# A causal mask as one rank-64 product of staircases instead of two 64-column products, in a transformer layer on one core

## The chip, the core and the metric

The kernel runs on one core of a Trainium2 chip. A core has a matrix engine (TensorE, PE in the profile; its weight loads are PEld), three engines for elementwise work (VectorE or DVE, ScalarE or ACT, GpSimd or POOL), and SyncE (SP), which here issues nearly all DMA transfers. Each engine works through its own list of instructions in order and waits on semaphores for the others. TensorE writes to PSUM only; the other data lie in SBUF. The metric is the device time of one execution in microseconds, as a median over runs.

## The reference

A transformer layer on two sequences of 2048 positions with 256 features: layer norm, causal attention with 16 heads of 16 features and rotary embedding, then layer norm and a gated feed-forward block with inner size 704, whose operands are rounded to a 4-bit grid in blocks of 16.

```python
q, k = (rope(q), rope(k))
scale = math.sqrt(HEAD_D)
att = jnp.einsum('bhqd,bhkd->bhqk', q, k) / scale
mask = jnp.tril(jnp.ones((t, t), dtype=bool))
att = jnp.where(mask, att, -jnp.inf)
att = jax.nn.softmax(att, axis=-1)
y = jnp.einsum('bhqk,bhkd->bhqd', att, v)
...
x = x + _L0_attn_ref(_layernorm(x, axis=-1), ...)
x = x + _L0_ffn_ref(_layernorm(x, axis=-1), ...)
```

Everything is float32. The part that matters here is the mask: a query may not see a later key.

## The kernel before

A sequence is cut into chunks of 512 positions (CH), four per sequence, each of four tiles of 128. The heads are taken in groups of four (GROUP), so there are 2 sequences x 4 chunks x 4 groups = 32 slots. Each slot runs two passes over the keys seen so far.

The maximum pass (`max_steps`) computes scores with queries on the partitions. A step is one query tile i, one key chunk kc and one pair of heads d: the two heads h lie in partitions 0 to 63 and 64 to 127 (`strips`, STRIP = 64), each with its query and key split into leading and trailing parts, so that a product contracts over 64 rows of the array. Both heads' products (L1094) go to two PSUM banks, and VectorE reduces each bank to a row maximum (L1118). Where the key chunk is the query's own, only (i + 1) x 128 columns are made, and the last 128 of them hold the causal triangle.

The exponential pass (`value_steps`) computes the scores again with keys on the partitions: a product that subtracts the maxima (L1227), the scores on top (L1235), and for the four key tiles of the chunk itself the triangle on the first 128 columns; ScalarE takes the exponential (L1250), and the values are multiplied with it (`weigh`, L1283), in column strips of 32.

The triangle is added on TensorE by `masked` (L1059). It accumulates on top of the scores a product of the triangle tile with a selecting identity. Since a strip has 64 rows, one product can select 64 columns, so each head takes two weight loads and two products of 64 columns (L1062). The tiles are `mask_q` for the maximum pass and `mask_k`, its mirror, for the exponential pass; both are bfloat16, filled with -1.0e30 or 0 by `triangle` on GpSimd (L377, L380) and narrowed on VectorE (L391). `pick` holds the two identities (L408).

The order of the whole program is laid by a planner. Each piece of work is added with an engine, an assumed cost, the things it reads and writes and a due time (`Plan.add`, L147), and `Plan.ordered` (L187) simulates the engines, keeps the buffers' limits (ROOM), and gives the sequence in which the pieces are written out; `in_order` (L505) then ties each engine to that sequence. The feed-forward steps of earlier chunks, the projections of the next chunk and the rounding of the weights are interleaved with the attention steps in this way. A different assumed cost can therefore move any piece. The planner also counts a penalty when TensorE changes between the tilings "strip" (64 rows), "value" (32 columns) and "whole".

In the first 170 us of the plan (KEPT), where the planner sees TensorE idle, `kept_busy` (L484) puts in filler products of 256 columns that have no use but to keep the engine running, one for each 0.2 us of planned idle time (FILLER). Their moving operand is `mask_q`, so none is put in before the planner sees that tile ready (L1901).

The set-up work of the start (`begun`, from L1831) has due times written by hand: `lay_mask_q` at -8.2, `lay_pick` at -8.1, `lay_mask_k` at -7.0 after the weights of the values.

Of the kernel before, what the change touches and what calls it, by code (L numbers as in the profile page):

```python
# [46 lines left out]
AUG = HD + 1  # L47
ROPE_BASE = 2500
LN_EPS = 1e-5
NEG = -1.0e30  # L50
CH = 512
TPC = CH // P
BLOCK = 16
# [261 lines left out]
def layer_kernel(  # L315
# [48 lines left out]
    make_identity(nc, ident)  # L364


    def triangle(name, sign):

        t, thing, full = const.tile([P, 2, P], BF16, name=name), Thing(), []

        def step(due, after=()):
            temp = Thing("x1")

            def filled():
                full.append(ffn.tile([P, E], F32, tag="x1", name="tri", bufs=ROOM["x1"]))
                wide = full[0].rearrange("p (h q) -> p h q", h=2)
                nc.gpsimd.memset(wide, 0.0)  # L377
                for strip in range(2):
                    part = wide[strip * STRIP : (strip + 1) * STRIP]
                    nc.gpsimd.affine_select(  # L380
                        out=part,
                        in_=part,
                        compare_op=ALU.is_ge,
                        fill=NEG,
                        base=0,
                        pattern=[[-sign * STRIP, 2], [sign, P]],
                        channel_multiplier=-sign,
                    )

            def narrowed():  # L390
                nc.vector.tensor_copy(t.rearrange("p h q -> p (h q)"), full[0])  # L391

            add(POOL, 1.2, filled, after, [temp], due)
            add(DVE, 0.33, narrowed, [temp], [thing], due)

        return t, thing, step


    mask_q, mask_q_, lay_mask_q = triangle("mask_q", 1)
    mask_k, mask_k_, lay_mask_k = triangle("mask_k", -1)  # L400
    pick = const.tile([P, STRIP], BF16, name="pick")
    pick_ = Thing()

    def lay_pick(due):
        def run():
            for strip in range(2):
                rows = slice(strip * STRIP, (strip + 1) * STRIP)
                nc.vector.tensor_copy(pick[rows], ident[rows, rows])  # L408

        add(DVE, 0.5, run, [fixed], [pick_], due)  # L410


    less = [const.tile([P, P], BF16, name=f"less{d}") for d in range(2)]
    less_ = Thing(), Thing()
# [69 lines left out]
    def kept_busy(bank):  # L484

        while spare[0] >= FILLER:
            spare[0] -= FILLER
            nc.tensor.matmul(
                bank[:, : 2 * P],
                lhsT=ident_b,  # L490
                rhs=mask_q.rearrange("p h q -> p (h q)"),
                start=True,
                stop=True,
            )
# [561 lines left out]
    def strips(t, h, *rest):  # L1056
        return t[(slice(STRIP * h, STRIP * (h + 1)), *rest)]

    def masked(sc, h, col, mask):  # L1059
        for half in range(2):  # L1060
            at = STRIP * half
            nc.tensor.matmul(  # L1062
                sc[h][:, col + at : col + at + STRIP],
                lhsT=strips(mask, h, half),
                rhs=strips(pick, h),
                start=False,
                stop=(half == 1),
            )

    order = [(b, c) for b in range(B) for c in range(NC)]  # L1070
    maxima, max_ = {}, {}
# [3 lines left out]
    def max_steps(b, c, g):  # L1075
# [7 lines left out]
        def one(i, kc, d, due):  # L1083
            duo = 2 * (g % 2) + d
            cols = CH if kc < c else (i + 1) * P
            ps, got = (Thing("ps"), Thing("ps")), []

            def run():
                qT = qTs[b, c, g]
                kT = kTs[b, kc, g // 2]  # L1090
                sc = [ps_s.tile([P, CH], F32, tag="ps", name="sc") for _ in range(2)]
                kept_busy(sc[0])
                for h in range(2):
                    nc.tensor.matmul(  # L1094
                        sc[h][:, :cols],
                        lhsT=strips(qT, h, d, slice(i * P, (i + 1) * P)),
                        rhs=strips(kT, h, duo, slice(0, cols)),
                        start=True,
                        stop=(kc < c),
                    )  # L1100
                if kc == c:
                    for h in range(2):
                        masked(sc, h, cols - P, mask_q)
                got.append(sc)

            def reduced(h):
                name = "parts" if c else "mx"
                if name not in st:
                    st[name] = att.tile(
                        [P, TPC, 2, 2, NC] if c else [P, TPC, 2, 2],  # L1110
                        F32,
                        tag=name,
                        name=name,
                        bufs=1 if c else 2,
                    )
                at = st[name][:, i, h, d]
                dst = at[:, kc : kc + 1] if c else at.unsqueeze(1)
                nc.vector.tensor_reduce(dst, got[0][h][:, :cols], AX.X, ALU.max)  # L1118

            add(  # L1120
                PE,
                0.18 + 0.44e-3 * cols if kc == c else 0.27,
                run,
                [qT_[b, c, g], k_[b, kc, g // 2][g % 2], mask_q_, pick_],
                [*ps, m_order],
                due,
                [parts if c else mx],
                "strip",
                FEED_M,
                0.07,  # L1130
            )
            for h in range(2):
                own = Thing(of=parts if c else mx)
                found.append(own)
                add(DVE, on_vector(cols), lambda h=h: reduced(h), [ps[h]], [own], due)
# [67 lines left out]
    def value_steps(b, c, g):  # L1203
# [9 lines left out]
        def score(j, d, due):  # L1213
            off = offset(j)
            duo = 2 * (g % 2) + d
            jj = (j % TPC) * P
            ps, got = (Thing("ps"), Thing("ps")), []
            ex_[j, d] = Thing("ex")

            def run():  # L1220
                qT = qTs[b, c, g]
                kT = kTs[b, j // TPC, g // 2]
                mT = maxima[b, c, g]
                sc = [ps_s.tile([P, CH], F32, tag="ps", name="sx") for _ in range(2)]
                kept_busy(sc[0])
                for h in range(2):
                    nc.tensor.matmul(  # L1227
                        sc[h][:, off:],
                        lhsT=strips(less[d], h),
                        rhs=strips(mT, h, slice(off, CH)),  # L1230
                        start=True,
                        stop=False,
                    )
                for h in range(2):
                    nc.tensor.matmul(  # L1235
                        sc[h][:, off:],
                        lhsT=strips(kT, h, duo, slice(jj, jj + P)),
                        rhs=strips(qT, h, d, slice(off, CH)),
                        start=False,
                        stop=(j < TPC * c),  # L1240
                    )
                if j >= TPC * c:
                    for h in range(2):
                        masked(sc, h, off, mask_k)
                got.append(sc)

            def exponential(h):
                if (j, d) not in st:
                    st[j, d] = exps.tile([P, 2, CH], F32, tag="ex", name="ex")
                nc.scalar.activation(  # L1250
                    st[j, d][:, h, off:], got[0][h][:, off:], AF.Exp, scale=HD**-0.5
                )

            cols = CH - off
            add(
                PE,
                0.455 if j < TPC * c else 0.14 + 0.75e-3 * cols,
                run,
                [qT_[b, c, g], k_[b, j // TPC, g // 2][g % 2], max_[b, c, g], mask_k_, pick_, less_[d]],
                [*ps, e_order],  # L1260
                due,
                [ex_[j, d]],
                "strip",
                FEED_V,
                0.22,
            )
            parts = ex_[j, d].parts = [Thing(of=ex_[j, d]) for _ in range(2)]
            for h in range(2):
                add(ACT, on_scalar(cols), lambda h=h: exponential(h), [ps[h]], [parts[h]], due)
# [574 lines left out]
    def transpose_biases(due):  # L1844
# [18 lines left out]
        (-8.6, lambda due: lay_bias(bvb, bv, bvb_, due)),  # L1863
        (0.4, lambda due: lay_bias(bob, bo, bob_, due)),
        (-8.8, lay_spread),
        (-8.2, lay_mask_q),
        (-8.1, lay_pick),
        (-7.3, lay_ident_b),
        (-7.2, lambda due: lay_less(0, due)),
        (-7.1, lambda due: lay_less(1, due)),  # L1870
        (-7.0, lambda due: lay_mask_k(due, [wv_])),
        (
            -7.6,
            lambda due: add(
# [23 lines left out]
        step(at)  # L1898
    plan.near_end = end - NEAR
    for t in plan.ordered():  # L1900
        if t.engine == PE and (t.end < KEPT or t.start > plan.span - ENDING) and ident_b_.there_by(t.start) and mask_q_.there_by(t.start):  # L1901
            spare[0] = t.idle
        t.run()
        spare[0] = 0.0
        in_order(t.end < DAWN)
# [62 lines left out]
```

## Time and profile before

| what | value |
|---|---|
| median of 3 runs | 1381.62 us (1381.47 to 1383.63) |
| span of the profiled execution | 1378.9 us |
| mean granted clock of TensorE | 0.979 of full speed |
| instructions of TensorE: products, weight loads | 10408, 10408 |
| of these L1062, the mask | 1024 in the maximum pass, 1024 in the exponential pass |
| fillers (L488) | 139, from 5.0 to 161.5 us |
| first scores product | 23.82 us |

The profiled execution is one run; its span goes from the first to the last instruction of the program. "Busy" of an engine is the union of its instructions' times; TensorE's products are pipelined, and each record lasts from its start to a modelled end, so records overlap. The chain is the work that ended last, followed back step by step to what released it. In the groups by form, a row gives line, engine, operation, names (written<-read), the tile of the array where it is not the whole (64*128 is 64 rows by 128 columns), the shape of the moving operand, the count, then busy time, mean duration in ns, and the idle time before. In the timeline, a row gives start and length in us, then engine, line, operation, names, shape, count, and the idle time before it with the releaser in brackets; equal neighbours are merged. In the table by stretch, a row gives the stretch, its length, then busy time and count for PE, PEld, DVE, ACT and POOL, the granted clock, the share of the DMA engines and GB/s.

### The profile page before, as it was taken

The page shows a single profiled execution, that of the slowest core. Times are in us where ns is not written, and L with a number is a line of the kernel's source. Part 1 is how long each engine was busy: PE and PEld are TensorE (multiplying, and loading weights), DVE is VectorE, ACT ScalarE, POOL GpSimd, SP SyncE. Part 2 cuts the span into 40 slices and gives each one's busy share as a digit, 9 for nine tenths or more (in the row PEclk, how much of TensorE's full clock was granted, in tenths as well). Part 3 has the DMA queues.
Part 4 walks back from the last instruction along what each step waited for, and adds up shares of the span by engine and source line. Part 5 has one row for each costly group of instructions (what it writes and reads, how often), then busy time and mean ns, then how long its engine had stood idle before and what let it go on. Part 6 is the DMA issues. An engine that isn't in the chain of part 4 may idle for free.

```text
span 1378.9 us, 27730 instructions
## 1 busy us (share of the span) xinstructions
PE 1317.6 (96%) x10408; PEld 656.7 (48%) x10408; DVE 1115.1 (81%) x2415; ACT 749.9 (54%) x1670; POOL 538.4 (39%) x685
## 2 busy tenths in 40 slices
PE   7988999999999999999998999999999999999977
PEld 4544444444544444444454555444454444444445
DVE  7788989988889998875479888996878988894296
ACT  2542655556555566557643455554655566667711
POOL 4754634434423334314345644432442332320360
PEclk8998999999999999999999999999999999999988
DMA  2653432411221401221343414240130130000000
GB/s 88 133 134 100 103 94 58 104 33 55 62 41 44 107 20 41 64 45 51 89 113 94 108 44 97 66 95 22 47 86 17 43 81 13 9 9 9 9 1 19
DMA packets 61887, 84.39 MB, mean 61 GB/s; under 512 B 14772, under 2 KB 30520, under 8 KB 61752
## 3 DMA queue, kind: packets, MB, share of 16 engines
q1 hardware_dynamic: 61744, 82.61, 24.2%
q8 instruction: 82, 1.34, 0.4%
q14 instruction: 53, 0.43, 0.1%
q10 hardware_dynamic: 8, 0.00, 0.0%
HBM read 55.09 MB, written 27.49 MB: 60 GB/s over the span
## 4 chain that ended last, share of the span: by engine, by line
PE 65%; DVE 19%; POOL 5%; issue 5%; DMA 3%; ACT 2%; SPq 0%; POOLq 0%; DVEq 0%; ACTq 0%
PE av L1283 15%; PE sc L1094 9%; PE pg L1575 9%; PE sx L1227 8%; DVE parts L1118 7%; PE sx L1235 7%; PE pd L1669 6%; PE pj L837 3%; PE pth L1434 2%; PE po L1519 1%; PE pv L1019 1%; DVE scale L582 1%; DVE step L609 1%; DVE mx L1118 1%; PE sc L1062 1%
## 5 line engine op out<-in xcount | busy, mean ns | idle before, releaser
L1250 ACT ACTIVATE ex<-sx 128x512 f32<-128x512 f32 (+3 forms) x1280 | 592.8, 538 | 345.9 <-PE sx L1235 202.1
L1118 DVE TENSOR_REDUCE parts<-sc 128x1 f32<-128x512 f32 (+3 forms) x1152 | 637.9, 611 | 65.2 <-PE sc L1094 46.6
L1235 PE MATMUL sx<-qT,kT 64*128 64x512 f32 (+3 forms) x1280 | 335.6, 521 | 0.0
L1283 PE MATMUL av<-ex,v 128*32 128x512 f32 (+3 forms) x2560 | 301.3, 543 | 0.0
L1094 PE MATMUL sc<-kT,qT 64*128 64x512 f32 (+3 forms) x1280 | 280.3, 425 | 8.9 <-DMA kT<-parts 2.5
L1227 PE MATMUL sx<-mT,less 64*128 64x512 bf16 (+3 forms) x1280 | 246.5, 355 | 5.4 <-DVE parts L1118 1.6
L1094 PEld LDWEIGHTS sc<-kT,qT 64*128 64x128 f32 x1280 | 132.8, 188 | 168.1 <-DVE parts L1118 51.2
L1227 PEld LDWEIGHTS <-less 64*128 64x128 bf16 x1280 | 66.5, 94 | 213.3 <-issue 205.5
L590 POOL TENSOR_SCALAR inv<-inv 128x16 f32<-128x16 f32 (+2 forms) x82 | 17.7, 216 | 373.0 <-DVE inv L586 341.2
L1235 PEld LDWEIGHTS sx<-qT,kT 64*128 64x128 f32 x1280 | 131.3, 196 | 9.0 <-issue 6.8
L1669 PE MATMUL pd<-wdT,hrT 128*128 128x256 f32 (+1 forms) x384 | 103.9, 411 | 1.5 <-ACT hrT L1438 1.0
L1283 PEld LDWEIGHTS av<-ex,v 128*32 128x32 f32 x2560 | 52.6, 108 | 70.8 <-issue 60.4
L1669 PEld LDWEIGHTS pd<-wdT,hrT 128*128 128x128 f32 (+1 forms) x384 | 70.4, 197 | 29.1 <-issue 16.0
L889 POOL TENSOR_TENSOR t<-t,cs 128x512 f32<-128x512 f32 x31 | 39.9, 1286 | 110.2 <-DVE t L883 104.8
L1575 PE MATMUL pg<-wgT,xT 128*128 128x352 f32 x224 | 76.9, 476 | 0.9 <-ACT xT L1438 0.8
L837 PE MATMUL pj<-xnT,wqkT 128*128 128x512 f32 x128 | 73.8, 672 | 3.5 <-DVE v L1028 1.7
L1118 DVE TENSOR_REDUCE mx<-sc 128x1 f32<-128x128 f32 (+3 forms) x128 | 54.3, 477 | 25.8 <-PE sc L1062 25.8
L1575 PE MATMUL pg<-wuT,xT 128*128 128x352 f32 x224 | 74.4, 471 | 0.1
L1062 PE MATMUL sc<-pick,mask_q 64*128 64x64 bf16 x1024 | 67.3, 198 | 0.0
L615 POOL TENSOR_TENSOR h<-h,step 128x704 f32<-128x704 f32 x28 | 47.2, 1686 | 48.8 <-DVE step L612 41.0
L1601 ACT ACTIVATE h<-pg 128x352 f32<-128x352 f32 x64 | 29.9, 467 | 64.6 <-PE pg L1575 56.5
L547 POOL TENSOR_SCALAR ve<-mv 128x1 f32<-128x1 f32 x64 | 12.6, 197 | 130.4 <-DVE mv L543 127.1
(163 smaller groups left out, 1614.8 us busy)
## 6 DMA issues: line engine op xcount, KB each, us to landing
qT<-parts SPq DMA_DIRECT2D x120, 128.0 KB
kT<-parts SPq DMA_DIRECT2D x120, 128.0 KB
parts<-high SPq DMA_DIRECT2D x30, 256.0 KB
parts<-t SPq DMA_DIRECT2D x30, 256.0 KB
sums<-avs SPq DMA_DIRECT2D x28, 256.0 KB
cs<-in_rope_dram SPq DMA_DIRECT2D x8, 512.0 KB
xin<-in_L_attn_x_dram SPq DMA_DIRECT2D x28, 128.0 KB
y<-sums SPq DMA_DIRECT2D x28, 128.0 KB
```

Source lines behind the costliest of these rows:

```text
L615: queue.tensor_tensor(src(), src(), st["step"], ALU.add)
L837: nc.tensor.matmul(got["pj"], lhsT=wqkT[:, k, i, cols], rhs=xnTs[b, c][:, k, :], start=(k == 0), stop=(k == KE - 1),)
L889: (nc.gpsimd if early and i == 0 else queue).tensor_tensor(swapped, swapped, angles[b, c][:, 1, :], ALU.mult)
L1062: nc.tensor.matmul(sc[h][:, col + at : col + at + STRIP], lhsT=strips(mask, h, half), rhs=strips(pick, h), start=False, stop=(half == 1),)
L1094: nc.tensor.matmul(sc[h][:, :cols], lhsT=strips(qT, h, d, slice(i * P, (i + 1) * P)), rhs=strips(kT, h, duo, slice(0, cols)), start=True, ...
L1118: nc.vector.tensor_reduce(dst, got[0][h][:, :cols], AX.X, ALU.max)
L1227: nc.tensor.matmul(sc[h][:, off:], lhsT=strips(less[d], h), rhs=strips(mT, h, slice(off, CH)), start=True, stop=False,)
L1235: nc.tensor.matmul(sc[h][:, off:], lhsT=strips(kT, h, duo, slice(jj, jj + P)), rhs=strips(qT, h, d, slice(off, CH)), start=False, stop=(j ...
L1250: nc.scalar.activation(st[j, d][:, h, off:], got[0][h][:, off:], AF.Exp, scale=HD**-0.5)
L1283: nc.tensor.matmul(st["av"][SLOT * s : SLOT * (s + 1), off:], lhsT=v[:, at : at + SLOT], rhs=st[j, d][:, h, off:], start=(j == 0), stop=(j ...
L1575: nc.tensor.matmul(got[half], lhsT=split("xrT")[:, k, :], rhs=wT[:, k, half * IH : (half + 1) * IH], start=(k == 0), stop=(k == KE - 1),)
L1669: nc.tensor.matmul(st["pd"], lhsT=st["hrT"][:n, k, :], rhs=wdT[:n, k, :], start=(k == 0), stop=(k == KI - 1),)
```

## The change

The two triangle tiles and the two identities are replaced by one bfloat16 tile `stairs` of two halves, for each strip of 64 rows. In row e, the first half, over positions q, is 2^80 for q <= 2e, 1 for q = 2e + 1, and 2^-80 beyond. The second half, over positions k, is -2^40 for k >= 2e + 2, -2^-40 for k = 2e + 1, and -2^-120 before. The product of the two, summed over the 64 rows, is at most -2^40 wherever k > q and between -2^-34 and 0 elsewhere. One product of 128 columns per head thus adds the whole triangle. In the maximum pass the first half is the stationary operand and the second the moving one; in the exponential pass they change places.

The tile is made by two memsets of 128 columns and eight selects of 64 x 128 on GpSimd, and one cast on VectorE, with due time -8.2. The fillers read `stairs`. The planner's assumed costs of a masked step fall by 0.065 us in the maximum pass and by 0.04 us in the exponential pass.

```diff
-NEG = -1.0e30
+STEEP = 80
+LOW = 40
...
-    def triangle(name, sign):
...
-    mask_q, mask_q_, lay_mask_q = triangle("mask_q", 1)
-    mask_k, mask_k_, lay_mask_k = triangle("mask_k", -1)
-    pick = const.tile([P, STRIP], BF16, name="pick")
-    pick_ = Thing()
-
-    def lay_pick(due):
-        def run():
-            for strip in range(2):
-                rows = slice(strip * STRIP, (strip + 1) * STRIP)
-                nc.vector.tensor_copy(pick[rows], ident[rows, rows])
-
-        add(DVE, 0.5, run, [fixed], [pick_], due)
-
+    stairs, stairs_ = const.tile([P, 2, P], BF16, name="stairs"), Thing()
+
+    def lay_stairs(due):
+
+        temp, flat = Thing("x1"), []
+        steps = (
+            (1, (2.0**STEEP, 1.0, 2.0**-STEEP), ((0, -1, 2), (1, -1, 2))),
+            (-1, (-(2.0**LOW), -(2.0 ** (LOW - STEEP)), -(2.0 ** (LOW - 2 * STEEP))), ((-2, 1, -2), (-1, 1, -2))),
+        )
+
+        def filled():
+            flat.append(ffn.tile([P, E], F32, tag="x1", name="flat", bufs=ROOM["x1"]))
+            both = flat[0].rearrange("p (n q) -> p n q", n=2)
+            for n, (_, (first, *fills), bounds) in enumerate(steps):
+                nc.gpsimd.memset(both[:, n, :], first)
+                for fill, (base, col, row) in zip(fills, bounds):
+                    for strip in range(2):
+                        part = both[strip * STRIP : (strip + 1) * STRIP, n, :]
+                        nc.gpsimd.affine_select(
+                            out=part,
+                            in_=part,
+                            compare_op=ALU.is_ge,
+                            fill=fill,
+                            base=base,
+                            pattern=[[col, P]],
+                            channel_multiplier=row,
+                        )
+
+        def narrowed():
+            nc.vector.tensor_copy(stairs.rearrange("p n q -> p (n q)"), flat[0])
+
+        add(POOL, 2.8, filled, [], [temp], due)
+        add(DVE, 0.33, narrowed, [temp], [stairs_], due)
...
-                rhs=mask_q.rearrange("p h q -> p (h q)"),
+                rhs=stairs.rearrange("p n q -> p (n q)"),
...
-    def masked(sc, h, col, mask):
-        for half in range(2):
-            at = STRIP * half
-            nc.tensor.matmul(
-                sc[h][:, col + at : col + at + STRIP],
-                lhsT=strips(mask, h, half),
-                rhs=strips(pick, h),
-                start=False,
-                stop=(half == 1),
-            )
+    def masked(sc, h, col, rows):
+
+        nc.tensor.matmul(
+            sc[h][:, col : col + P],
+            lhsT=strips(stairs, h, rows),
+            rhs=strips(stairs, h, 1 - rows),
+            start=False,
+            stop=True,
+        )
...
-                        masked(sc, h, cols - P, mask_q)
+                        masked(sc, h, cols - P, 0)
...
-                0.18 + 0.44e-3 * cols if kc == c else 0.27,
+                0.115 + 0.44e-3 * cols if kc == c else 0.27,
...
-                        masked(sc, h, off, mask_k)
+                        masked(sc, h, off, 1)
...
-                0.455 if j < TPC * c else 0.14 + 0.75e-3 * cols,
+                0.455 if j < TPC * c else 0.1 + 0.75e-3 * cols,
...
-        (-8.2, lay_mask_q),
-        (-8.1, lay_pick),
+        (-8.2, lay_stairs),
...
-        (-7.0, lambda due: lay_mask_k(due, [wv_])),
```

More of the change, by code (lines that the diff above doesn't have):

```diff
@@ L364, in layer_kernel @@
     make_identity(nc, ident)
-    def triangle(name, sign):
[L369 to L377, printed above, removed]
-                for strip in range(2):
[L379 to L387, printed above, removed]
-                    )
[L390 to L396, printed above, removed]
@@ L399, in layer_kernel @@
-    mask_q, mask_q_, lay_mask_q = triangle("mask_q", 1)
-    mask_k, mask_k_, lay_mask_k = triangle("mask_k", -1)
-    pick = const.tile([P, STRIP], BF16, name="pick")
-    pick_ = Thing()
-    def lay_pick(due):
-        def run():
-            for strip in range(2):
-                rows = slice(strip * STRIP, (strip + 1) * STRIP)
-                nc.vector.tensor_copy(pick[rows], ident[rows, rows])
-        add(DVE, 0.5, run, [fixed], [pick_], due)
+    stairs, stairs_ = const.tile([P, 2, P], BF16, name="stairs"), Thing()
@@ L1057, in strips @@
         return t[(slice(STRIP * h, STRIP * (h + 1)), *rest)]
-    def masked(sc, h, col, mask):
-        for half in range(2):
-            at = STRIP * half
-            nc.tensor.matmul(
-                sc[h][:, col + at : col + at + STRIP],
-                lhsT=strips(mask, h, half),
-                rhs=strips(pick, h),
-                start=False,
-                stop=(half == 1),
-            )
+    def masked(sc, h, col, rows):
[6 more added lines that the diff above has]
+        )
     order = [(b, c) for b in range(B) for c in range(NC)]
@@ L1121, in one @@
                 PE,
-                0.18 + 0.44e-3 * cols if kc == c else 0.27,
+                0.115 + 0.44e-3 * cols if kc == c else 0.27,
                 run,
-                [qT_[b, c, g], k_[b, kc, g // 2][g % 2], mask_q_, pick_],
+                [qT_[b, c, g], k_[b, kc, g // 2][g % 2], stairs_],
                 [*ps, m_order],
@@ L1256, in score @@
                 PE,
-                0.455 if j < TPC * c else 0.14 + 0.75e-3 * cols,
+                0.455 if j < TPC * c else 0.1 + 0.75e-3 * cols,
                 run,
-                [qT_[b, c, g], k_[b, j // TPC, g // 2][g % 2], max_[b, c, g], mask_k_, pick_, less_[d]],
+                [qT_[b, c, g], k_[b, j // TPC, g // 2][g % 2], max_[b, c, g], stairs_, less_[d]],
                 [*ps, e_order],
@@ L1900, in layer_kernel @@
     for t in plan.ordered():
-        if t.engine == PE and (t.end < KEPT or t.start > plan.span - ENDING) and ident_b_.there_by(t.start) and mask_q_.there_by(t.start):
+        if t.engine == PE and (t.end < KEPT or t.start > plan.span - ENDING) and ident_b_.there_by(t.start) and stairs_.there_by(t.start):
             spare[0] = t.idle
```

## The prediction

> **What bounds the kernel now.** I read the page's busy times and chain first, then the groups of TensorE by form, then the timeline around one causal tile, the first 12 us, and last the busy time by stretch.
>
> ```profile
> span 1378.9 us, 27730 instructions
> PE 1317.6 (96%) x10408; PEld 656.7 (48%) x10408; DVE 1115.1 (81%) x2415; ACT 749.9 (54%) x1670; POOL 538.4 (39%) x685
> PE 65%; DVE 19%; POOL 5%; issue 5%; DMA 3%; ACT 2%; SPq 0%; POOLq 0%; DVEq 0%; ACTq 0%
> ```
>
> The span is 1378.9 us; the median of the runs, 1381.62 us, is 2.7 us more, and I carry those 2.7 us over. TensorE (PE) is busy for 96% and holds 65% of the chain that ended last; VectorE (DVE) has 19%. So a nanosecond taken from TensorE's stream should mostly be a nanosecond of the end, except where another engine feeds it late.
>
> ```profile
> L1227 PE MATMUL sx<-mT,less 64*128 64x512 bf16 x896 | 188.8, 387 | 4.1 <-DVE parts L1118 1.6 <-ACT ex L1250 0.7 <-ACT mT L1179 0.7
> L1062 PE MATMUL sc<-pick,mask_q 64*128 64x64 bf16 x1024 | 67.3, 198 | 0.0
> L1062 PE MATMUL sx<-pick,mask_k 64*128 64x64 bf16 x1024 | 62.8, 197 | 0.0
> L1227 PE MATMUL sx<-mT,less 64*128 64x128 bf16 x128 | 15.6, 221 | 1.3 <-DVE mx L1118 0.8 <-ACT ex L1250 0.4
> ```
>
> 2048 mask products, four to a step (two heads, two halves of 64 columns), so 512 masked steps: 256 in the maximum pass and 256 in the exponential pass. The durations of 198 ns are mostly pipeline latency, since they overlap; what a step costs is read from starts:
>
> ```profile
> 55.66 0.33 PE L1062 MATMUL sx<-pick,mask_k 64*128 64x64 bf16 x4
> 55.80 0.61 PE L1227 MATMUL sx<-mT,less 64*128 64x512 bf16 x2
> 57.18 0.23 PE L1062 MATMUL sx<-pick,mask_k 64*128 64x64 bf16 x4
> 57.25 0.33 PE L1227 MATMUL sx<-mT,less 64*128 64x384 bf16 x2
> 57.28 0.47 PE L1235 MATMUL sx<-qT,kT 64*128 64x384 f32 x2
> 57.59 0.23 PE L1062 MATMUL sx<-pick,mask_k 64*128 64x64 bf16 x4
> 57.76 1.50 PE L1283 MATMUL av<-ex,v 128*32 128x512 f32 x8
> ```
>
> From the first mask product to the next work is 0.07 us (57.18 to 57.25). It is 0.17 us where the next product has another tiling (57.59 to 57.76), and 0.14 us on a slow clock (55.66 to 55.80). The two heads sit in different halves of the array's rows and run side by side, so the 0.07 us are two 64-column products, one after the other.
>
> **The mask products.** Each head's two weight loads and two products become one load and one product of 128 columns. The price of a column comes from the L1227 rows: (387 - 221) ns / 384 columns = 0.43 ns, so 128 columns stream in 55 ns. Against 70 ns that is 15 ns saved, times 512 steps 7.7 us. The durations give a second reading: four products last 0.23 us from first start to last end, one product of this shape 0.221 us, 9 ns less, 4.6 us in all. I take 7.7 us. Bounds: below, nothing, because 2 x 64 columns are the same 128 columns; above, the second product disappears whole and each strip keeps one product of some 0.03 us, so 0.04 us x 512 = 20 us.
>
> Two rules of the Trainium skill pull in opposite directions, and neither enters the sum. "TensorE: Matmul & The Clock Gate", section "Back-to-back issue gap", puts up to 64 columns at about 60 cycles and 128 columns at 134; at its 2.4 GHz two small products are 50 ns and the large one 56 ns, so by it the change would lose 6 ns a step, about 3 us as an estimate. The trace stands against that: two small products take 70 ns, not 50. "TensorEngine Tiling (Array Packing)", section "Instruction Overhead", charges some 60 cycles for every product whatever its size; by it, one product fewer in each strip saves 25 ns a step, an estimate of 12.8 us. No row here shows the 128-column mask product itself.
>
> How much of it reaches the end depends on the stretch:
>
> ```profile
> 26.00:100.00 74.00, 66.27 (x604) 34.95 (x604) 56.55 (x151) 31.21 (x78) 44.82 (x65) 0.88 0.48 114
> 700.00:800.00 100.00, 93.36 (x764) 53.04 (x762) 87.54 (x201) 43.51 (x108) 58.03 (x70) 0.97 0.43 103
> ```
>
> The first number after the length is TensorE's busy time. At the opening of each batch, where nearly every tile is causal, it idles 7.7 us of 74 and 6.6 us of 100. About a fifth of the mask products lie there, and I let them count for little; with 0.85 for the whole, 7.7 us become **-6.5 us**. The cover that takes the rest is the feeding of TensorE by DVE and the transfers in these two stretches; if that cover were gone, all 7.7 would count.
>
> **The start.** Two triangles become one tile of staircases, made on GpSimd (POOL) before the first normalization.
>
> ```profile
> 2.69 0.31 POOL L377 MEMSET tri<- 128x256 f32 x1
> 3.07 0.90 POOL L380 TENSOR_SCALAR_AFFINE_SELECT tri<-tri 64x256 f32<-64x256 f32 x2
> 5.70 0.19 POOL L547 TENSOR_SCALAR ve<-mv 128x1 f32<-128x1 f32 x1 [1.72 <-DVE mv L543]
> 1.32 1.93 DVE L408 CAST pick<-ident 64x64 bf16<-64x64 f32 x2 [1.32 <-POOL ident masks.py:199]
> 4.69 0.28 DVE L391 CAST mask_q<-tri 128x256 bf16<-128x256 f32 x1
> 5.02 2.51 PE L488 MATMUL ptx<-mask_q,ident_b 128*128 128x256 bf16 x11 [1.76 <-DVE mask_q L391]
> 7.32 0.63 PE L767 MATMUL ptx<-ident,first 128*128 128x128 f32 x2
> ```
>
> The first triangle takes POOL 1.28 us (2.69 to 3.97). The staircases take two 128-column memsets (0.20 us each in the rows of the tile flat) and eight selects of 64 x 128. Their nearest rows are the 128 x 128 select of the identity, 0.29 us, and the 64 x 256 ones, 0.45 us; both bounds together give 2.7 to 4.0 us, and I take 2.7, since the free size, 128, is the identity's. POOL is done at 5.4 us. The four variance powers of the first normalization are queued behind it on POOL, but the first of them began only at 5.70, waiting for DVE, and DVE loses the 1.93 us of casts to pick from its head; so the normalization starts no later (0.3 us earlier at best). On DVE the cast of the staircases stands ahead of the first normalization and waits for POOL, but that normalization waits for POOL anyway.
>
> What does come late is the row of filler products on TensorE that keep its clock up, because they read the staircases: ready at about 5.7 us instead of 4.97, and in the built order 13 of them instead of 11 before the first transpose. At 2.51/11 = 0.23 us each they end at 8.7 us, where the last row above shows the transposes from 7.32, effectively 7.53. That is up to 1.2 us on the way to the first projection; ScalarE's chain of copies behind it has a gap of 0.48 us. I take **+1.0 us**, bounds -0.3 and +1.2 (+2.5 with the dearer selects). The second triangle (1.25 us of POOL from 11.43, a 0.28 us cast on DVE) falls away for nothing: POOL idles 5.39 us after it.
>
> **The order.** The planner has new costs for the 512 steps (0.065 us less in one pass, 0.04 in the other), so the order is laid again. In the built program 85% of TensorE's products, masks aside, keep their place in a common sequence, and the last 1225 of 6303 are identical: the end of the kernel is untouched. The changes of tiling on TensorE go from 1144 to 1154; each costs 0.17 - 0.07 = 0.10 us: **+1.0 us**. Fillers go from 139 to 158, 17 of them after the start. At 0.21 us each, which is a filler's pace on the slow clock, that is 3.6 us if none falls into idle time, and I put half there: +1.8. They also hold up the clock, granted at 0.88 from 26 to 100 us; full speed would be worth up to 0.12 x 66 = 8 us there, and 14% more fillers might bring 14% of it: -1.1. Together **+0.7 us**, bounds -8 and +3.6. No transfer is added; the queues keep their 570 issues on SP, in a slightly different sequence.
>
> **Sum.** -6.5 + 1.0 + 1.0 + 0.7 = -3.8 us: a span of 1375.1, a time of **1377.8 us**, -0.28%.
>
> **Rivals.** A measurement here tells a change from none at about 0.2%, 2.8 us: below 1378.9 is faster, above 1384.4 slower.
> *The mask step nearly disappears.* If the single product hides wholly behind its neighbours, the upper bound of 20 us holds: 1381.6 - 20 + 2.7 = 1364. For it: 15 ns rests on a streaming rate, while the weight loads (98 ns of record each, 2048 of them) also go to half. Against it: 128 columns must pass, 55 ns by the L1227 slope. Chance 0.12; the forecast itself 0.40.
> *Nothing gained.* The stream is the same 128 columns, the second small product was hidden already, and the start, the tilings and the fillers cost their 2.7 us, so between 1379 and 1384, about 1382. For it: the bound of zero and the mere 9 ns of the second reading. Against it: 0.07 us are visible between starts, more than 55 ns. Chance 0.20.
> *The new order makes a new wait, slower.* The place is the opening of the second batch (700 to 800 us), where the chain holds 4.14 us of a transfer into xin and 3.12 us of one into x, and DVE is busy 87.5 us of 100. If the new order puts TensorE in front of one such pair again, 7.3 us come on top: 1385. It decides from 6.6 us of new TensorE idle time on (1384.4 - 1377.8). For it: 15% of the products move. Against it: those transfers are issued well ahead by SP, and the length of the queue is unchanged. Chance 0.28.
>
> **The numbers.** Faster 0.40 + 0.12 = 0.52, no difference 0.20, slower 0.28. The range of 1365 to 1388 takes in most of the first rival and of the third with a second such wait; the forecast's own range is 1372 to 1379.
>
> **What would show it.** L1062's successor: 1024 products of 64 x 128 near 221 ns, and 0.055 to 0.06 us from a mask to the next strip product. The first projection at 12.4 us instead of 11.39. TensorE's idle time about 61 us as now. It is wrong if the mask-to-next distance stays at 0.07, if it falls to 0.03, or if 700 to 800 us shows TensorE below 90.

## The result, and the profile after

The changed kernel takes 1403.15 us (median of 4 runs, 1400.77 to 1406.5) beside 1382.62 us for the kernel before: a ratio of 1.0137, 95% interval [1.0112, 1.0162]. It is slower by 1.4%. The profiled execution has a span of 1401.0 us (its run took 1402.82) and a granted clock of 0.969, where before had 1378.9 us and 0.979. The page's own totals of the changed kernel, and its chain by engine:

```profile
span 1401.0 us, 25697 instructions
...
PE 1327.1 (95%) x9403; PEld 656.2 (47%) x9403; DVE 1116.4 (80%) x2412; ACT 749.3 (53%) x1670; POOL 537.1 (38%) x689
...
PE 68%; DVE 21%; DMA 4%; POOL 3%; ACT 2%; issue 2%; SPq 1%; POOLq 0%; DVEq 0%; ACTq 0%
```

The span grew by 22.1 us. TensorE's idle time (span less busy) went from 1378.9 - 1317.6 = 61.3 us to 73.9 us, 12.6 more. Its busy time grew too, by 9.5 us, with fewer products in it. The clock tells why: span x (1 - granted clock) is a measure of the time lost to a clock at half speed, and it went from 1378.9 x 0.021 = 29.0 us to 1401.0 x 0.031 = 43.4 us, 14.4 more. What is left of the span after both is 1288.6 us before and 1283.7 after, and between 1283 and 1291 in all the profiles below. So the loss is idle TensorE and a slow clock, not more work.

The mask products among the groups by form (line, operation, count, busy us, mean ns):

```profile
L1050 PE MATMUL sc<-stairs 64*128 64x128 bf16 x512 | 67.8, 233 | 0.0
...
L1050 PE MATMUL sx<-stairs 64*128 64x128 bf16 x512 | 61.4, 231 | 0.0
```

There are 1024 where there were 2048, each 12 and 10 ns longer than the 221 ns of its nearest row. What a step costs is again the distance from the mask's start to the next start. Two places on the full clock, in the timeline of the changed kernel:

```profile
219.83 0.23 PE L1050 MATMUL sx<-stairs 64*128 64x128 bf16 x2
219.90 0.22 PE L1215 MATMUL sx<-mT,less 64*128 64x128 bf16 x2
...
750.12 0.23 PE L1050 MATMUL sc<-stairs 64*128 64x128 bf16 x1
750.16 0.30 PE L1082 MATMUL sc<-kT,qT 64*128 64x128 f32 x1
```

Ahead of a bfloat16 product (219.83 to 219.90) it is 0.07 us, as before; over all such pairs the typical distance went from 68 to 66 ns. Ahead of a float32 scores product (750.12 to 750.16) it is 0.04 us, typically 39 ns where it was 68. In the changed kernel's order 159 mask steps stand ahead of the first kind, 116 ahead of the second, 104 ahead of the values in their other tiling (163 ns went to 160), and 133 ahead of whole-array products and fillers, which I count like the values. That makes 159 x 2 + 116 x 29 + 237 x 3 ns = 4.4 us, an estimate of what the product gives.

The start, TensorE and GpSimd in the timeline:

```profile
2.97 1.35 POOL L386 TENSOR_SCALAR_AFFINE_SELECT flat<-flat 64x128 f32<-64x128 f32 x4
...
4.66 1.35 POOL L386 TENSOR_SCALAR_AFFINE_SELECT flat<-flat 64x128 f32<-64x128 f32 x4
...
6.38 2.93 PE L477 MATMUL ptx<-stairs,ident_b 128*128 128x256 bf16 x13 [3.04 <-DVE stairs L397]
...
13.07 3.70 PE L826 MATMUL pj<-xnT,wqkT 128*128 128x512 f32 x8 [0.39 <-ACT xnT L762]
...
26.00 0.47 PE L1082 MATMUL sc<-kT,qT 64*128 64x128 f32 x2 [0.23 <-ACT qT L985]
```

A 64 x 128 select takes 1.35 / 4 = 0.34 us, so GpSimd is done at 6.01 and not at 5.4. The fillers start at 6.38, the first projection at 13.07 (11.39 before), the first scores at 26.00 (23.82 before): 2.2 us late.

The two stretches in which the changed kernel loses most, by stretch (length, then busy time of PE, PEld, DVE, ACT and POOL, clock, DMA share, GB/s); first 200 to 300 us in the kernel before, then both in the changed one:

```profile
200.00:300.00 100.00, 96.95 (x766) 47.05 (x764) 92.78 (x197) 52.65 (x116) 45.48 (x54) 1.00 0.34 76
```

```profile
200.00:300.00 100.00, 93.14 (x644) 44.47 (x640) 88.06 (x192) 52.63 (x114) 44.52 (x53) 0.97 0.35 78
...
700.00:800.00 100.00, 87.78 (x587) 51.36 (x586) 76.54 (x181) 39.14 (x100) 47.87 (x59) 0.90 0.43 104
```

TensorE idles 6.9 us of the first hundred (3.0 before) and 12.2 of the second (6.6 before). The end of each slot is marked by ScalarE's copy of its sums (L1293, 32 of them). Against the kernel before that copy is 2.3 us late in the first slot, 5 in the sixth, 11.6 in the seventh, 10 to 18 until the nineteenth, 10 early in the twentieth, which the new order ends sooner, 22.3 late in the twenty-first, at the opening of the second batch, and 24 in the last.

What stands in these places, first GpSimd, VectorE and TensorE around the seventh slot:

```profile
217.34 0.73 POOL L1491 TENSOR_TENSOR x<-x,bob 128x256 f32<-128x256 f32 x1 [3.46 <-DMA x<-in_L_attn_x_dram]
...
221.50 0.29 DVE L598 TENSOR_SCALAR step<-xn 128x256 int32<-128x256 int32 x1 [2.53 <-POOL h L607]
...
226.50 1.51 PE L1422 MATMUL pth<-ident,h 128*128 128x128 f32 x6 [3.67 <-DVE parts L1106]
```

GpSimd's bias addition stands in its list ahead of the rounding of h and waits 3.46 us for its transfer. VectorE stands 2.53 us for that rounding, with row maxima (parts) queued behind it. TensorE's next product, the transpose of h, starts only at 226.50; by the profile it was such a row maximum that released it, so the delay reached TensorE by way of VectorE. VectorE and TensorE at the opening of the second batch:

```profile
752.38 0.25 DVE L1348 RECIPROCAL den<-den 128x16 f32<-128x16 f32 x1 [7.32 <-DMA den<-sums]
...
753.36 0.77 PE L1082 MATMUL sc<-kT,qT 64*128 64x512 f32 x3 [2.44 <-DVE parts L1106]
...
784.01 0.61 PE L1163 MATMUL ptm<-ident_b,mslots 128*128 128x128 bf16 x4 [3.65 <-DVE mslots L1147]
```

VectorE stands 7.32 us before a reciprocal of 16 columns whose input is still on its way, with the maxima queued behind it, and TensorE soon has no free bank. 31 us later TensorE waits 3.65 us for the split maxima. The clock in the stretches around these stalls:

```profile
225.00:236.00 11.00, 9.50 (x48) 6.66 (x48) 8.03 (x19) 3.03 (x7) 3.11 (x3) 0.69 0.10 37
...
778.00:792.00 14.00, 8.65 (x31) 5.58 (x31) 13.72 (x30) 3.18 (x7) 9.49 (x12) 0.52 0.16 49
```

It is granted at 0.69 and 0.52. Each stall is paid twice: once as idle time and once in the products next to it that run at half speed.

### The profile page after: what moved, and what is told of

The parts are those of the page before. It is cut to its first block, busy times and chain, and to the rows that moved or that the text cites. A ratio compares the mean times of both kernels' runs of the same rounds, so it can differ in the third digit from the quotient of the medians.

```text
span 1401.0 us, 25697 instructions
## 1 busy us (share of the span) xinstructions
PE 1327.1 (95%) x9403; PEld 656.2 (47%) x9403; DVE 1116.4 (80%) x2412; ACT 749.3 (53%) x1670; POOL 537.1 (38%) x689
## 4 chain that ended last, share of the span: by engine, by line
PE 68%; DVE 21%; DMA 4%; POOL 3%; ACT 2%; issue 2%; SPq 1%; POOLq 0%; DVEq 0%; ACTq 0%
PE av L1271 15%; PE sc L1082 10%; PE pg L1563 9%; PE sx L1215 9%; DVE parts L1106 8%; PE sx L1223 7%; PE pd L1657 6%; PE pj L826 3%; PE pth L1422 2%; PE pv L1008 1%; PE po L1507 1%; DVE mx L1106 1%; DMA kT<-parts 1%; DVE step L601 1%; ACT ex L1238 1%
## 5 line engine op out<-in xcount | busy, mean ns | idle before, releaser
L1082 PE MATMUL sc<-kT,qT 64*128 64x512 f32 (+3 forms) x1280 | 283.4, 429 | 15.0 <-DVE parts L1106 8.8
L1082 PEld LDWEIGHTS sc<-kT,qT 64*128 64x128 f32 x1280 | 135.7, 191 | 176.4 <-DVE parts L1106 64.3
L1050 PEld LDWEIGHTS <-stairs 64*128 64x128 bf16 x1024 | 55.3, 95 | 54.6 <-issue 34.1
L1050 PE MATMUL sc<-stairs 64*128 64x128 bf16 x512 | 67.8, 233 | 0.0
L1589 ACT ACTIVATE h<-pg 128x352 f32<-128x352 f32 x64 | 29.7, 465 | 69.9 <-PE pg L1563 61.3
```

The costliest lines, as they stand in the source:

```text
L1050: nc.tensor.matmul(sc[h][:, col : col + P], lhsT=strips(stairs, h, rows), rhs=strips(stairs, h, 1 - rows), start=False, stop=True,)
L1082: nc.tensor.matmul(sc[h][:, :cols], lhsT=strips(qT, h, d, slice(i * P, (i + 1) * P)), rhs=strips(kT, h, duo, slice(0, cols)), start=True, ...
```

## The experiments

The question was which of three things costs the 20 us: the product, the start, or the order that the planner lays. Each ratio is against the kernel before on the same chip, with its 95% interval.

**The product and the order apart.** `e1` has the single product, but its pieces are presented to the planner as the old ones (old costs, the old set-up pieces, of which two do nothing), so the order is that of before. `e2` is the kernel before with the new assumed costs alone. `e3` is the changed kernel with the old costs. `e4` is the changed kernel with the costs that the measured distances call for.

```diff
# e1, against the changed kernel
-        add(POOL, 2.8, filled, [], [temp], due)
-        add(DVE, 0.33, narrowed, [temp], [stairs_], due)
+        add(POOL, 1.2, filled, [], [temp], due)
+        add(DVE, 0.33, narrowed, [temp], [mask_q_], due)
...
+        add(DVE, 0.5, lambda: None, [fixed], [pick_], due)
...
# e2, against the kernel before
-                0.18 + 0.44e-3 * cols if kc == c else 0.27,
+                0.115 + 0.44e-3 * cols if kc == c else 0.27,
...
-                0.455 if j < TPC * c else 0.14 + 0.75e-3 * cols,
+                0.455 if j < TPC * c else 0.1 + 0.75e-3 * cols,
# e3, against the changed kernel: 0.115 back to 0.18, 0.1 back to 0.14
# e4, against the changed kernel: 0.115 to 0.17, 0.1 to 0.13
```

> The single 128-column product and the staircases in exactly the order of before: the planner gets the old tasks and the old costs, the identity copies and the second triangle become empty. Theory A (the loss is the new order, the product itself gains a little): between 1374 and 1382 us; the mask's distance to the next strip product as in the changed kernel (0.066 us before L1227's like, 0.04 before a scores product), which over the 512 steps is worth 4 to 5 us, less about 2 us for the later start. Theory B (the product or the staircases themselves cost the time, in PSUM or in the loads): near 1400 us in spite of the old order.

> The kernel before with nothing changed but the two assumed costs of a masked step (0.115 for 0.18, 0.1 for 0.14): old products, old start, and on every engine nearly the order of the changed kernel. Theory A (the order): 1402 to 1410 us, as slow as the changed kernel or a few us slower, with the same lost time at the openings of the chunks (about 4 us by the fifth slot, 8 us more at the second batch). Theory B (the product): 1381 to 1385 us.

> The changed kernel with the old assumed costs (0.18, 0.14) and all else changed: staircases in the planner's start, single product. Its order differs from that of before in a few places of the first microseconds. Theory A: 1374 to 1382 us, like the first run of this set within 2 us. Theory B: near 1400 us.

> The changed kernel with assumed costs that fit what its trace shows of a masked step, 0.17 and 0.13, that is 10 ns less than before. This gives a third order. If only the size of the assumed saving misleads the planner (theory A1), this is at least as good as the old order, 1372 to 1382 us. If any new order is a draw (theory A2), it may fall anywhere between 1375 and 1400 us.

Measured: `e1` 1383.28 us, ratio 0.9994 [0.9978, 1.0009]. `e2` 1401.71 us, 1.013 [1.01, 1.016]. `e3` 1382.07 us, 0.9984 [0.9965, 1.0003]. `e4` 1406.87 us, 1.017 [1.014, 1.02]. In the built programs the order of `e2` shares 6300 of TensorE's 6303 products (masks aside) with the changed kernel, and that of `e3` all but 2 with the kernel before. By stretch, `e2` first, then `e3`:

```profile
700.00:800.00 100.00, 89.81 (x737) 53.06 (x737) 75.86 (x176) 39.37 (x101) 46.94 (x57) 0.86 0.43 110
```

```profile
700.00:800.00 100.00, 92.96 (x634) 52.79 (x634) 85.65 (x198) 41.94 (x104) 57.30 (x70) 0.95 0.42 102
```

The old product in the new order has the loss (TensorE idles 10.2 us, clock 0.86); the new product in the old order has not (7.0 us, 0.95, against 6.6 and 0.97 before). The four corners settle it: with either product the new order costs 1.3 to 1.4%, which is the whole loss. The product with its start makes -0.06% (`e1`) or -0.16% (`e3`) in the old order and +0.07% in the new one (1.0137 beside 1.013), which these runs can't tell from nothing. `e4` shows that nearer costs don't bring the good order back.

`e8` asks whether any move of the costs loses. It is the kernel before with both costs up by 0.01.

```diff
-                0.18 + 0.44e-3 * cols if kc == c else 0.27,
+                0.19 + 0.44e-3 * cols if kc == c else 0.27,
...
-                0.455 if j < TPC * c else 0.14 + 0.75e-3 * cols,
+                0.455 if j < TPC * c else 0.15 + 0.75e-3 * cols,
```

> The kernel before, old products, with assumed costs 10 ns higher (0.19 and 0.15): another order, one that errs on the side of a slow TensorE. If only costs below the true ones do harm (theory A1), it stays within 3 us of before. If an order is a draw whichever way the costs move (theory A2), it is likely slower by 5 to 25 us.

Measured: 1387.94 us, 1.0028 [1.001, 1.0046], 4.5 us more than the kernel before on that chip, between what the two theories expected. Ten nanoseconds of assumed cost make a difference of 0.3%.

**The waits.** `e5` keeps the changed kernel's order of TensorE and moves three waiting pieces back in their own engines' lists: the reciprocals that stood 4.87 us (at 109 us) and 7.32 us (at 752 us) by 12 and 10 pieces, the bias addition at 217 us by 6. `e7` tells the planner that the sums for the reciprocals land 6 us later (SLACK), so that the whole order is laid anew around it. `e9` does the same to `e4`, `e10` to the kernel before, and `e11` adds the same allowance for the bias addition's transfer.

```diff
# e5
-    for t in plan.ordered():
+    for t in moved_back(plan.ordered(), (('den', 2, 12), ('bias', 2, 6), ('den', 18, 10))):
# e7, e9, e10
-            add(SP, landing(8) , dens, [sums_], [den_], due)
+            add(SP, landing(8) + SLACK, dens, [sums_], [den_], due)
# e11, on top of e7
-            add(SP, landing(128), run, [], [things["x0"]], due - 1.0 * last)
+            add(SP, landing(128) + SLACK, run, [], [things["x0"]], due - 1.0 * last)
```

> The changed kernel with its own costs and order, except three pieces of work that stood in their engine's queue waiting for a transfer: the reciprocal of the denominators in the third slot (VectorE waited 4.87 us at 109 us) and in the nineteenth (7.32 us at 752 us), put 12 and 10 VectorE pieces later, and the addition of the output bias to the third tile (GpSimd waited 3.46 us at 217 us), put 6 GpSimd pieces later; what hangs on them directly moves along. TensorE's own order is not touched. Theory A (these in-order waits starve TensorE, and TensorE's clock then halves for about 7 us each): the idle times of 2.97 us at 113, 3.67 us at 226 and 2.44 us at 753 go, and the half clock after them mostly; 8 to 16 us less, 1387 to 1395 us. Theory C (the loss is spread over the new TensorE order itself): 1400 to 1404 us.

> The changed kernel where the planner is told that the denominators land 6 us later than it assumed (the slack that it already gives to the transfer after them); nothing else. A new order in which VectorE should not wait for them: their waits fall from 20.6 us in 7 to under 6 us. Theory A: faster than the changed kernel by 5 to 15 us, 1388 to 1398 us, unless the new order puts other waits in their place (the bias, kT), in which case 1395 to 1410.

> The order drawn with the costs 0.17 and 0.13 (24 us slower than before in its run), with the denominators' landing assumed 6 us later and nothing else changed. If the planner's too early landing of the denominators is the cause of the loss in general (theory A), and not a draw that the changed kernel happened to win when this landing was altered (theory A2), this falls by 15 to 27 us as well, to 1376 to 1390 us. By A2 it may stay near 1400.

> The kernel before, old products and costs, with the denominators' landing assumed 6 us later. Its waits for them were only 4.6 us in all, so by theory A there is little to win: 1380 to 1388 us, within 4 us of before. It is the control for the value of the single product: against it the changed kernel with the same landing has the same freedom from these waits.

> The changed kernel with the denominators' landing assumed 6 us later, and also the landing of the tiles to which GpSimd adds the output bias, for which it still waited 18.5 us in 6 places in the run with the first alone. Theory A: these waits go, and with them up to 5 us: 1374 to 1381 us. If GpSimd's waits there cost TensorE nothing, it stays within 3 us of the run with the denominators alone (1380.9).

Measured: `e5` 1396.76 us, 1.0095 [1.0069, 1.0121]. `e7` 1380.86 us, 0.9987 [0.997, 1.0005]. `e9` 1396.45 us, 1.0085 [1.0055, 1.0115]. `e10` 1406.7 us, 1.0158 [1.0123, 1.0193]. `e11` 1385.18 us, 1.0004 [0.9985, 1.0024]. The rows of the waits for these transfers, first the changed kernel, then `e5` (total us, times, longest):

```profile
DVE den L1348 <- DMA den<-sums: 20.6, 7, 7.3
...
POOL x L1491 <- DMA x<-in_L_attn_x_dram: 13.3, 7, 3.5
```

```profile
DVE den L1367 <- DMA den<-sums: 11.7, 6, 2.6
...
POOL x L1510 <- DMA x<-in_L_attn_x_dram: 9.4, 6, 2.6
```

Three moved pieces bring back about 6 of the 20 us, with an uncertainty of some 5; that lies between the two expectations of `e5`. After `e7` it looked as if the landing assumed too early was the whole cause: with it right, the changed kernel is level with before. That theory fell with the next runs. In `e9` no reciprocal waits for its sums any more, and half the loss stays; in `e10` the same repair makes the good order of before 1.6% slower. `e7` was one more lucky order, and `e11` on top of it gains nothing. Nor do the totals of such waits tell a good order: GpSimd's waits for x and for its other transfer (over) are 18.5 and 16.8 us in `e7`, which is level with the kernel before, 13.3 and 9.7 in the changed kernel and 7.8 and 15.5 before; in `e10` they are 18.3 and 29.4.

**The two orders spliced.** To ask where an order loses without drawing a third one, both orders are laid in one program, and the sequence follows the one as far as a planned time and then the other. At the cuts the two had placed nearly the same pieces (at most 5 were held over), so nothing had to be put off. All have the single product.

```diff
+    (a, ta, span), (b, tb, _) = laid(plan, first_other), laid(plan, not first_other)
+    n = next((n for n, t in enumerate(a) if ta[t][2] >= cut), len(a))
+    out, done = a[:n], set(a[:n])
...
+    rest = [t for t in b if t not in done]
...
-    for t in plan.ordered():
+    for t in spliced(plan, FIRST_OTHER, CUT):
# e13: new order to 550 us, then old    e14: old to 550, then new
# e15: new to 800, then old             e16: old to 800, then new
# e17: e14 with ("den", 18, 10) moved back as in e5
# e18: new to 130, then old
```

> All four kernels have the single product and the staircases of the changed kernel; only the sequence is spliced. This one follows the changed kernel's order as far as planned time 550 us (some 585 us of the chip's), then the order that the old costs give. If every stretch of an order has its own price, this loses what the changed kernel had lost by then, 11 to 14 us: 1393 to 1398. If the loss at the opening of the second batch only follows from entering it late, the full loss comes: 1400 to 1406. If the early loss is made good later: 1380 to 1385.

> The old costs' order as far as planned time 550 us, then the changed kernel's. If every stretch has its own price, this loses the 8 to 12 us that the changed kernel loses at the opening of the second batch: 1390 to 1396. If that loss follows from entering late, nothing: 1380 to 1385.

> The changed kernel's order as far as planned time 800 us, past the opening of the second batch, then the old costs' order. Slots after that lost 2 us, so by the slots the full loss less some 2 us: 1399 to 1406. If something in the rest of the order matters, visibly less: below 1395.

> The old costs' order as far as planned time 800 us, then the changed kernel's. By the slots nothing of the loss, or some 2 us: 1380 to 1387. If something in the rest of the order matters: above 1390.

Measured: `e13` 1392.54 us, 1.0073 [1.0049, 1.0098]. `e14` 1392.69 us, 1.0061 [1.0034, 1.0088]. `e15` 1400.36 us, 1.012 [1.0087, 1.0153]. `e16` 1381.52 us, 0.9986 [0.9964, 1.0008]. `e13` lost a little less than was expected from the slots, `e14` what was expected. The two halves add up within their uncertainty: 0.73 + 0.61 = 1.34%, against 1.37% of the changed kernel. Past planned time 800 us the new order costs nothing. By stretch, `e13` first, then `e14`:

```profile
200.00:300.00 100.00, 93.46 (x644) 44.60 (x644) 88.19 (x189) 51.24 (x113) 44.41 (x54) 0.97 0.34 77
...
700.00:800.00 100.00, 92.65 (x632) 52.11 (x631) 82.20 (x193) 41.53 (x101) 47.88 (x59) 0.95 0.50 113
```

```profile
200.00:300.00 100.00, 97.34 (x670) 45.92 (x667) 90.77 (x193) 53.08 (x116) 46.78 (x55) 0.98 0.34 76
...
700.00:800.00 100.00, 88.16 (x578) 49.90 (x577) 81.69 (x187) 37.49 (x91) 50.64 (x61) 0.90 0.43 101
```

The idle time goes with the order: 6.5 and 7.3 us in `e13`, 2.7 and 11.8 in `e14`, where the changed kernel has both, 6.9 and 12.2. The opening of the second batch in `e14`, entered some 9 us earlier, repeats the changed kernel's stalls almost to the hundredth:

```profile
743.56 0.25 DVE L1417 RECIPROCAL den<-den 128x16 f32<-128x16 f32 x1 [7.37 <-DMA den<-sums]
```

```profile
744.54 0.97 PE L1151 MATMUL sc<-kT,qT 64*128 64x512 f32 x3 [2.42 <-DVE parts L1175]
...
774.09 0.61 PE L1232 MATMUL ptm<-ident_b,mslots 128*128 128x128 bf16 x4 [3.65 <-DVE mslots L1216]
```

So the second loss isn't the echo of the first. Two last runs look for the wait behind each.

> The old-then-new splice at planned time 550 us, with one piece moved: the reciprocal of the nineteenth slot's sums, which stood 7.37 us before its transfer at 736 us, goes behind ten more pieces of VectorE. If that wait is what the opening of the second batch costs, most of the 8.4 us come back: 1383 to 1386. If the opening's other waits (1.73 us on the partial maxima, 3.65 us on the split maxima) cost as much by themselves, about half: 1387 to 1390. If the piece costs nothing: 1391 to 1394.

> The changed kernel's order as far as planned time 130 us only (some 150 us of the chip's), then the old costs' order, so without the stretch in which GpSimd's bias addition waits 3.46 us at 214 us. If that stall is the larger part of the first loss (8.5 us of the new-then-old splice at 550 us), this takes 1384 to 1388. If the loss lies ahead of 150 us, 1390 to 1395.

Measured: `e17` 1391.73 us, 1.0043 [1.0026, 1.006]; `e18` 1386.03 us, 1.0011 [0.9995, 1.0026]. TensorE at the opening in `e17`, and the stretch:

```profile
768.87 1.26 PE L1170 MATMUL sc<-kT,qT 64*128 64x512 f32 x3 [1.73 <-DVE parts L1194]
...
775.17 0.61 PE L1251 MATMUL ptm<-ident_b,mslots 128*128 128x128 bf16 x4 [3.65 <-DVE mslots L1235]
```

```profile
700.00:800.00 100.00, 89.55 (x587) 50.85 (x586) 82.32 (x184) 38.92 (x94) 49.56 (x60) 0.90 0.45 105
```

The 7.37 us wait of VectorE is gone, and the 2.42 us of TensorE that hung on it; the ratio is 0.2 points lower than that of `e14`, with intervals that overlap, and TensorE's idle time in the hundred fell from 11.8 to 10.5 us. So the longest wait of the opening cost some 2 of the 8 us and was probably not its main cost; the two intervals together would allow up to 7, so this isn't shown. The 3.65 us wait and the slow clock (0.90 in the hundred, as in `e14`) stand as they were. `e18` puts the first loss behind planned time 130 us: 1.0011 with the new order until there, 1.0073 with it until 550. That fits the stall at 217 to 226 us, which lies between; it doesn't prove that it is that stall alone.

**The start.** `e6` is `e1` with GpSimd filling one half of the tile and VectorE making the other as its scaled reciprocal. `e12` is `e7` with the staircases laid late (and assumed to take 3.4 us), and fillers that read the bfloat16 identity in their place.

```diff
# e6
+            nc.vector.reciprocal(second, first)
+            nc.vector.tensor_scalar(stairs[:, 1, :], second, -(2.0 ** (LOW - STEEP)), None, ALU.mult)
# e12
-        (-8.2, lay_stairs),
+        (-7.0, lambda due: lay_stairs(due, [wv_])),
...
+                    bank[:, n * P : (n + 1) * P], lhsT=ident_b, rhs=ident_b, start=True, stop=True
```

> The old order with the single product, as in the first run of the first set, and the staircases made in half the GpSimd work: GpSimd fills the first half alone (one memset, four selects, 1.7 us for 3.4), VectorE makes the second as -2^-40 divided by it. If the later start (first scores product 1.4 to 2.1 us later than before) is what ate the product's gain, the first scores product comes at about 24.2 us and the time is 2 to 4 us under before, a ratio of 0.997 to 0.9985. If the product gains nothing, the ratio is 0.999 to 1.001.

> A try at a version that beats both: the changed kernel with the denominators' landing assumed 6 us later, the staircases laid behind the first normalization on GpSimd (they are needed only at 24 us), and the fillers reading the identity, two of 128 columns for each one of 256, none before the first transpose of the biases. The first scores product should come at 23 to 24.5 us instead of 25.9: 1376 to 1381 us, a ratio of 0.996 to 0.999.

Measured: `e6` 1381.64 us, 0.9989 [0.9974, 1.0004], first scores at 24.53 us where `e1` has 25.23. `e12` 1383.49 us, 0.9982 [0.9965, 1.0]; its first scores come at 25.94 us and not at 23 to 24.5 as expected, so it doesn't show what an earlier start is worth. The start's 1 to 2 us are at the edge of what shows, and neither version beats the kernel before by more than its uncertainty; nor does any other version here.

## Why the prediction was wrong

*The order* is the step that failed. It was priced at +1.0 us for ten more changes of tiling and +0.7 us for fillers and clock, and the bounds of -8 and +3.6 us held nothing else. Measured alone (`e2`) it costs 1.3%, some 17 to 18 us. The count of tilings says nothing of it: where the trace shows the loss, it shows pieces that stand in an in-order engine's list ahead of a transfer or of another engine's late result, and a half-speed clock around TensorE's pauses. That these waits make the whole loss is argued, not shown: with the longest of them moved, `e5` won back about 6 of 20 us and `e17` some 2 of 8. I saw that 15% of the products move and priced the 15% by two of their properties.

*The third rival* had the kind of wait, the place (700 to 800 us) and the check (TensorE below 90; it is 87.78). Its price was wrong: 7.3 us were one pair of waits, taken from the chain of the old order. There were two losses of 8 to 10 us in two places (`e13`, `e14`), and the first, at 200 to 300 us, had no row before to be read from. Its argument against itself, that transfers are issued well ahead, looked at the issue and not at who stands in line for the landing. The waits that came were for the sums of the reciprocals and for x, 4.6 and 7.8 us in all before, 20.6 and 13.3 after.

*The mask products* were mis-sized: -6.5 us forecast, 4.4 us at most by the distances. 70 ns were to become 55 everywhere; they became 66 ahead of a bfloat16 product and 39 ahead of a float32 one. The streaming rate was the wrong measure in both cases. By an estimate from the table in "Back-to-back issue gap" of "TensorE: Matmul & The Clock Gate" in the Trainium skill, the large product would cost 6 ns more than two small ones. None of the three measured distances got longer; the table gives one gap for a size, while here the gap depended on what came next.

*The start*: +1.0 us forecast with 12.4 us for the first projection; it came at 13.07, since a select takes 0.34 us and not 0.29, and the first scores 2.2 us late. The first normalization, forecast no later, had its first variance power on GpSimd at 6.09 us where it was at 5.70. The dearer bound, named as +2.5, was nearer. With the 4.4 us above, the net of product and start should be some -2 us; `e1`, `e3` and `e16` have 0.9994, 0.9984 and 0.9986, all with intervals that reach 1.

*The idle time* of about 61 us as before was forecast and is 73.9. *"Nothing gained"*, the second rival, is what the change does by itself, in the old order.

Shown by runs: the order is the whole loss, it has two separate places (between planned times 130 and 550 us, and between 550 and 800), and the part after 800 us is innocent. Not settled: which of the waits decides in either place. At the opening of the second batch the 7.37 us one gave back some 2 of 8 us; the 3.65 us before the split maxima and the half clock around it are the next candidates, and they weren't taken out alone. Nor is it known what, short of running it, tells a good order: the eight re-laid ones of these runs lie between 0.9982 and 1.017. Five of them (the changed kernel, `e4`, `e8`, `e9`, `e10`) are clearly slower than the kernel before, three (`e7`, `e11`, `e12`) are level, none is clearly faster: the order of before stands at the good end of the spread, so that a new one was likely to lose.

## What to carry to other kernels

Where a planner lays a static order, a changed cost is a new draw of the whole order: build the change once in the old order and the old change-free work once in the new order, before anything is read into the time. Price a re-laid order by the spread of other orders of the same kernel, here -0.2% to +1.7%, and not by counts of what the planner optimizes. Splicing two orders at a planned time tells where one of them loses, without drawing a third.

## What the runs showed of the hardware

The gain of a smaller mask step depended on its successor: 2 ns ahead of a bfloat16 product of the same tiling, 29 ns ahead of a float32 one, 3 ns ahead of another tiling. Stretches at half clock stood around TensorE's pauses. The clock was 0.50 from 225.55 to 232.38 us, around the end of a pause of 3.67 us; 0.50 from 754.62 to 761.44 us, after a pause of 2.44 us; and 0.50 from 778.51 to 792.16 us, which began after a pause of 1.73 us and ahead of the one of 3.65 us. "HAM oscillation — how this bites in real kernels" in "TensorE: Matmul & The Clock Gate" of the Trainium skill puts the limit at pauses above some 3.4 us. The first case agrees with it; the other two began after shorter pauses, and there the measurement decides. In `e6` a VectorE reciprocal of 128 x 128 float32 took 0.95 us, more than two of GpSimd's selects of 64 x 128 at 0.34 us.
